# A new order of preparation work beside the products of a two-layer Flamingo-style kernel

## The chip, the cores and the metric

The kernel runs on one core of one Trainium2 chip. The metric is device time in microseconds (us), the median of repeated runs of the whole program. The engines are TensorE (PE in the profile, its weight loads PEld), VectorE (DVE), ScalarE (ACT) and GpSimd (POOL); SyncE (SP) issues nearly all transfers.

## What is computed

Four batches of 512 tokens, 512 channels wide, pass through two layers. Layer 0 adds a cross attention over normalised scores and a GELU network whose weights are first rounded to a 4-bit format with one power-of-two scale for each block of 32. Layer 1 adds a causal attention of 16 heads and a gated network whose hidden vector goes through a Walsh-Hadamard transform.

```python
x = x + tanh(g_xattn[0]) * L0_xattn(layernorm(x), ctx)
x = x + tanh(g_ffn[0]) * (gelu(layernorm(x) @ q4(up) + b) @ q4(down) + b2)
x = x + tanh(g_xattn[1]) * softmax(mask(q k^T / sqrt(32))) v Wout^T
h = silu(n @ W1^T) * (n @ W3^T);  x = x + tanh(g_ffn[1]) * fwht(h) @ W2^T
```

The transform is moved onto the weights: W2 is transformed once instead of every hidden vector. Products are made of two-part numbers (`hi`, `lo`), so one product is two or three matmuls for each pair of tiles.

## The kernel before

**Stages.** The cross attention of layer 0 fills the first 119 us. Then come the GELU products, `ffn0` (lines 579 to 632): the hidden dimension is cut into 16 chunks of 128 in four groups of 512 (`wq4[n]` holds one group's rounded weights, and two groups fit at a time). A call `ffn0(groups, b, beside)` runs the chunks of these groups for batch `b`: for each chunk eight `pu` matmuls (line 135), two GELUs on ACT, the subtraction `glo` on DVE (line 617), and for the chunk before it eight `acc` matmuls (line 594). The last 16 chunks are in `ffn0_end` (from 1026), where PE's order is the order of the program (`manual_schedule`). Then the attention of layer 1 in 16 units of four heads (loop over `s`, from 1573, one step `s` a head), and the gated network in 16 steps `n` (from 1797), in both of which PE keeps the program's order too. Elsewhere, and on all other engines, a planner orders instructions: it simulates the program with its own costs and gives each engine the earliest traced instruction that it believes ready.

**Work beside the products.** Preparations are Python generators. `work(k, jobs)` runs the next `k` steps of the first generator in a list. In `ffn0` each chunk runs `beside[0]` steps of `weight_jobs` and `beside[1]` of `jobs`, inside `with behind(traced())`: each instruction made there may not stand on its engine ahead of that engine's last instruction so far. That holds for PE, DVE, ACT and POOL; transfers are not held.

**Rounding.** `quantise(n)` (485 to 569) rounds group `n` in 11 steps: one that issues the loads of the raw weights into two half tiles `qw0` and `qw1`, one for each half that finds block scales (line 525 and a tree of maxima at 531), then four pairs of steps that round a quarter each (549 to 559). After the second and fourth pair a half is stored to `qw_d` (566). The next group's loads into a half wait for that store. `fetch_q(n)` (571) loads the rounded group back from `qw_d` as `up_q` and `dn_q`.

**W2 transform.** `hadamard_w2(c)` (953) takes ten steps for a quarter of W2: a load into `fw`, eight butterfly steps (an addition and a subtraction on DVE, lines 283 and 284), a store to `w2_d`. Two tiles `fw0` and `fw1` alternate, so the next quarter's first butterfly needs its own load and the store before it. `last_weights` (five steps) transposes Wq with PE, ACT and DVE. `preparations()` (1083) strings these together: four steps of quarter 0, rounding of group 2, the rest of quarter 0, rounding of group 3, `last_weights`, quarters 1 to 3: 62 steps in all.

**`ffn0_end`.** A list `plan` tells for each of the 16 chunks which jobs run before and after the chunk's `acc` matmuls: `A` is the first attention unit (queries of batch 0, then the largest scores of unit 0), `B` the queries of batch 1, `C` those of batch 2, `W` the preparations. The queries begin with a layer norm: statistics and scale on DVE (a step), the first rows `xn_c` on ACT (line 243, a step), then PE transposes (259), four steps.

**Attention.** `maxima(n)` (394) finds each row's largest score: score matmuls (410), for the two narrow row blocks with a mask added by a matmul (415) and one reduction (419), for the wide ones one reduction with mask for each head (423); then `mhi` on ACT and a transpose `pm` (435), whose rows are sent to the stacked operands. It is 13 steps, 11 of them scores. The narrowest row block takes four heads in its first step. Three steps run in each `s`; unit `u = (s + 7) // 4` starts where `k = (s + 7) % 4` is 0. The operands of unit n + 3 are loaded two heads at a time, after heads 1 and 3 of unit n (`load_heads`, 321). The exponentials need the largest scores of their unit.

Once for each batch the sums of the exponentials go to memory and back as reciprocals (`shares`, 1449: `den_d`, `rden`, `rden_d`, `rows_d`); `divide` (1493) spreads them by a matmul `rep` (1498) and multiplies on DVE, and `finish` (1504) multiplies by Wout.

**Norms of the gated network.** `norm(b)` (1249) takes the statistics of `x[b]` (194, 195) and a scale by twelve small DVE instructions (207 to 223). `combine` (1257) needs them for its rows. Norms 0 and 1 are traced at `s = 52`, norms 2 and 3 at step `n = 6` of the gated network.

Of the kernel before, what the change touches and what calls it, by code (L numbers as in the profile page):

```python
# [42 lines left out]
def flamingo_kernel(  # L43
# [350 lines left out]
    def maxima(n, masks, bank, bank_m, junk, mr):  # L394

        qst, kst = stacks[n]
        mask, mx, tri = masks  # L400
        fin = small.tile([P, NT, 4], F32, tag="fin", name=f"fin{n}")
        junk = junk(f"junk{n}")
        for i in range(NT):
            w = (i + 1) * P
            per = max(1, 4 // (i + 1)) if i < 2 else 1
            for g0 in range(0, 4, per):
                sc = bank([P, per, w], f"sc{n}_{i}_{g0}")
                masked = per > 1
                for g in range(per):
                    nc.tensor.matmul(  # L410
                        sc[:, g, :], qst[:96, g0 + g, ts(i, P)], kst[:96, g0 + g, :w],
                        start=(g == 0 or not masked), stop=not masked,
                    )
                if masked:
                    nc.tensor.matmul(  # L415
                        sc[:, :, w - P :], tri[:, 0], tri[:, 1].unsqueeze(1).to_broadcast([P, per, P]),
                        start=False, stop=True
                    )
                    nc.vector.tensor_reduce(fin[:, i, g0 : g0 + per], sc, AX.X, ALU.max)  # L419
                    yield  # L420
                    continue
                for g in range(per):
                    nc.vector.tensor_tensor_reduce(  # L423
                        junk[:, :w], sc[:, g, :], mask[:, S - w :], 1.0, -3.0e38,
                        ALU.add, ALU.max, fin[:, i, g0 + g : g0 + g + 1],
                    )
                yield
# [12 lines left out]
        yield  # L440
# [16 lines left out]
    with ExitStack() as l0:  # L457
# [121 lines left out]
        def ffn0(groups, b, beside=(0, 0), between=None):  # L579
# [8 lines left out]
            chunks = [4 * n + j for n in groups for j in range(4)]  # L588

# [11 lines left out]
            for f in chunks:  # L601
# [19 lines left out]
                with behind(traced()):  # L621
                    work(beside[0], weight_jobs)
                    work(beside[1])
# [10 lines left out]
        with ExitStack() as xa:  # L634
# [289 lines left out]

            def fetched(n):
                fetch_q(n)
                yield
# [17 lines left out]
            ffn0((0,), 0, (2, 5))  # L945
# [4 lines left out]
        with ExitStack() as ff:  # L950
# [132 lines left out]
            def preparations():  # L1083


                q = [quantise(n) for n in range(NG)]
                h = [hadamard_w2(c) for c in range(ND)]
                last = last_weights()
                next(q[2])
                yield from some(4, h[0])  # L1090
                yield from q[2]
                fetch_q(2)
                next(q[3])
                yield from some(6, h[0])
                next(h[1])
                yield from q[3]
                fetch_q(3)
                yield from last
                yield from some(8, h[1])
                next(h[2])  # L1100
                yield from h[1]
                yield from some(8, h[2])
                next(h[3])
                yield from h[2]
                yield from h[3]

            weight_jobs.append(preparations())
# [6 lines left out]
            ffn0((2, 3), 0, (1, 0))  # L1114
# [16 lines left out]
            with tc.manual_schedule(engines={nc.tensor.engine}):  # L1131
# [13 lines left out]
    with ExitStack() as l1:  # L1145
# [187 lines left out]
        with ExitStack() as at:  # L1333
# [238 lines left out]
            with tc.manual_schedule(engines={nc.tensor.engine}):  # L1572
                for s in range(-3, 4 * last + 2):
# [32 lines left out]
                    for i in range(3):  # L1606
# [36 lines left out]
                    if s > 20 and s % 16 == 6:  # L1643
                        jobs.append(finish(n // NO - 1))
# [255 lines left out]
```

## Time and profile before

| | us |
|---|---|
| three runs | 1315.11, 1318.45, 1318.72 |
| median | 1318.45 |
| profiled execution, its own time | 1317.84 |
| its span, first to last instruction | 1316.1 |
| busy: PE, DVE, ACT, POOL | 1217.1, 844.9, 553.7, 354.6 |

The span is shorter than the time by 1.7 us, and the profiled execution is 0.6 us under the median. The mean granted TensorE clock is 0.963 of full speed. A timeline line reads: start, duration, engine, line of the kernel, operation, output and inputs, shape, count, and in brackets the idle time before it with what ended it. A waits line reads: who waited for whom, us in total, times, longest. A windows line reads: stretch, its length, busy us of PE, PEld, DVE, ACT and POOL with counts, granted clock, share of DMA engines, GB/s.

### The profile page before, as it was taken

To read this page: it belongs to the slowest core of one execution; us is meant where nothing else is said; L and a number is where in the kernel's file an instruction comes from. 1 tells how busy PE (TensorE), PEld (TensorE's weight loads), DVE (VectorE), ACT (ScalarE), POOL (GpSimd) and SP (SyncE) were. 2 spreads that over 40 slices of the span, in tenths; PEclk is the share of its full clock that TensorE was granted. 3 is DMA by queue.
4 is the path that set the end of the run, shared out by engine and by line. 5 is a ranking of instruction groups with operands and counts; after the bars stand their busy time and mean duration, and the time that the engine had idled before them with its cause. 6 is when DMAs were issued, how large, how long until landed. Compare 5 with 4: busy or idle time off the path is not lost. (4 is left out here: it accounts for less than half of the span.)

```text
span 1316.1 us, 17489 instructions
## 1 busy us (share of the span) xinstructions
PE 1217.1 (92%) x6081; PEld 910.2 (69%) x6081; DVE 844.9 (64%) x1756; ACT 553.7 (42%) x1040; POOL 354.6 (27%) x480
## 2 busy tenths in 40 slices
PE   5998799998898899897999788999999999999998
PEld 4645577886676775464655466777777788888886
DVE  4977888795567674464564468666666755455556
ACT  4559642333423454444463755333334642222210
POOL 0000020000000133444444325344444533333330
PEclk9999899998899899899988989999999999999999
DMA  9792273713224565445341027344453644543421
GB/s 185 285 245 95 88 168 56 201 49 96 88 92 125 178 191 149 119 122 151 90 147 38 10 82 288 132 170 177 176 192 130 246 176 146 180 162 144 146 87 64
DMA packets 113202, 186.43 MB, mean 142 GB/s; under 512 B 13228, under 2 KB 65580, under 8 KB 107994
## 3 DMA queue, kind: packets, MB, share of 16 engines
q1 hardware_dynamic: 110754, 185.04, 44.7%
q8 instruction: 48, 0.79, 0.2%
q10 hardware_dynamic: 2360, 0.28, 0.2%
q14 instruction: 40, 0.33, 0.1%
HBM read 109.22 MB, written 75.80 MB: 141 GB/s over the span
## 5 line engine op out<-in xcount | busy, mean ns | idle before, releaser
L135 PE MATMUL pS<-tok,pack 128*128 128x512 f32 x768 | 195.0, 399 | 0.0
L135 PE MATMUL acc<-w2T,gg 128*128 128x512 f32 x768 | 182.1, 391 | 0.6 <-DVE x L1774 0.5
L135 PEld LDWEIGHTS pS<-tok,pack 128*128 128x128 f32 x768 | 142.7, 189 | 32.9
L135 PEld LDWEIGHTS acc<-w2T,gg 128*128 128x128 f32 x768 | 143.3, 188 | 31.8 <-DVE x L1774 1.9
L135 PE MATMUL pA<-tok,pack 128*128 128x512 f32 x576 | 149.7, 397 | 0.0
L135 PE MATMUL pu<-xnT,up_q 128*128 128x512 f32 x512 | 136.1, 411 | 7.4 <-DMA up_q<-qw_d 5.5
L1774 DVE SCALAR_TENSOR_TENSOR x<-acc,tg,x 128x512 f32<-128x512 f32 x128 | 96.2, 751 | 67.7 <-PE acc L135 67.4
L1392 ACT ACTIVATE e<-sT 128x384 f32<-128x384 f32 (+1 forms) x192 | 95.5, 527 | 75.2 <-PE sT L1388 72.9
L135 PEld LDWEIGHTS pA<-tok,pack 128*128 128x128 f32 x576 | 106.7, 188 | 23.8
L135 PEld LDWEIGHTS pu<-xnT,up_q 128*128 128x128 f32 x512 | 99.7, 197 | 32.4 <-DMA up_q<-qw_d 5.9
L1398 POOL TENSOR_SCALAR_AFFINE_SELECT e<-e 128x128 f32<-128x128 f32 (+1 forms) x192 | 63.2, 331 | 151.6 <-ACT e L1392 146.9
L423 DVE CUSTOM_DVE_ANT_0 junk<-sc,mask 128x384 f32<-128x384 f32 (+1 forms) x128 | 79.4, 620 | 27.8 <-PE sc L410 20.1
L410 PE MATMUL sc<-stk 96*128 96x128 f32 (+3 forms) x256 | 79.3, 359 | 11.8 <-DMA stk<-k_d 9.3
L1815 ACT CAST gg<-s 128x512 fp32r<-128x512 f32 x64 | 39.7, 621 | 108.5 <-POOL s L1812 95.7
L1812 POOL TENSOR_TENSOR s<-s,p 128x512 f32<-128x512 f32 x15 | 19.6, 1308 | 238.8 <-DVE p L1810 162.8
L1388 PE MATMUL sT<-stk 98*128 98x512 f32 (+3 forms) x256 | 78.1, 361 | 2.6 <-ACT e L1392 1.6
L594 PE MATMUL acc<-dn_q,glo 128*128 128x512 f32 x192 | 76.4, 398 | 3.8 <-DVE glo L617 3.8
L1816 POOL TENSOR_TENSOR gg<-s,gg 128x512 fp32r<-128x512 f32 x60 | 77.0, 1297 | 5.0 <-ACT gg L1815 4.8
L613 ACT ACTIVATE ghi<-pu,up_b 128x512 fp32r<-128x512 f32 x48 | 33.0, 688 | 103.9 <-PE acc L594 95.4
L594 PE MATMUL acc<-dn_q,ghi 128*128 128x512 f32 x192 | 75.9, 396 | 0.0
L419 DVE TENSOR_REDUCE fin<-sc 128x2 f32<-128x512 f32 (+1 forms) x48 | 32.6, 687 | 65.6 <-PE sc L415 65.3
L1388 PEld LDWEIGHTS sT<-stk 98*128 98x128 f32 x256 | 47.0, 199 | 30.9 <-issue 10.8
(291 smaller groups left out, 2226.4 us busy)
## 6 DMA issues: line engine op xcount, KB each, us to landing
pack_d<-pack SPq DMA_DIRECT2D x16, 1024.0 KB
pack<-pack_d SPq DMA_DIRECT2D x16, 1024.0 KB
pack_d<-pack SPq DMA_DIRECT2D x16, 768.0 KB
pack<-pack_d SPq DMA_DIRECT2D x16, 768.0 KB
qw_d<-qw SPq DMA_DIRECT2D x64, 128.0 KB
q_d<-qq SPq DMA_DIRECT2D x16, 512.0 KB
st<-in_L_ffn_W_dram SPq DMA_DIRECT2D x32, 256.0 KB
w2T_d<-w2T SPq DMA_DIRECT2D x16, 512.0 KB
```

Of the source, the lines that this page charges most:

```text
L135: nc.tensor.matmul(out, a, b, start=(i == 0), stop=(i == len(terms) - 1))
L410: nc.tensor.matmul(sc[:, g, :], qst[:96, g0 + g, ts(i, P)], kst[:96, g0 + g, :w], start=(g == 0 or not masked), stop=not masked,)
L419: nc.vector.tensor_reduce(fin[:, i, g0 : g0 + per], sc, AX.X, ALU.max)
L423: nc.vector.tensor_tensor_reduce(junk[:, :w], sc[:, g, :], mask[:, S - w :], 1.0, -3.0e38, ALU.add, ALU.max, fin[:, i, g0 + g : g0 + g + 1],)
L594: nc.tensor.matmul(acc[t], g[:, ts(t, P)], dn[:, f % 4, :], start=(f == chunks[0] and i == 0), stop=(f == chunks[-1] and i == 1 and groups ...
L613: nc.scalar.activation(ghi, ph, AF.Gelu_apprx_tanh, bias=up_b[:, f : f + 1])
L1388: nc.tensor.matmul(sc[:, at_ : at_ + S - j * P], kst[:98, g, ts(j, P)], qst[:98, g, j * P :], start=True, stop=True,)
L1392: nc.scalar.activation(e[:, ds(EOFF[js[0]], w)], sc, AF.Exp)
L1398: nc.gpsimd.affine_select(diag, diag, [[0, len(js)], [1, P]], ALU.is_ge, 0.0, base=0, channel_multiplier=-1,)
L1774: nc.vector.scalar_tensor_tensor(x[b][:, t, :], acc, tg[:, 3:4], x[b][:, t, :], ALU.mult, ALU.add)
L1815: nc.scalar.copy(g[:, 0], s)
L1816: eng.tensor_sub(g[:, 1], s, f32(g[:, 0]))
```

## The change

1. The first `ffn0` call runs one step of the rounding of group 1 for each chunk instead of two. So four of its twelve steps (with the fetch) move into the third call, and `preparations` begins in the fourth.
2. `in_order` ties the preparations: each step's DVE instructions stand behind the last DVE instruction of the step before.
3. `preparations` has a new order: two steps of quarter 0, group 2, three steps of quarter 0, group 3, the rest of quarter 0, `last_weights`, then quarters 1 to 3, each followed by an empty step; 65 steps. The last `ffn0` call takes two steps for each of its first five chunks. `ffn0_end` has a new plan: no `W` before the fifth chunk, the first transposes of `A` a chunk later, `B` started two chunks earlier and its transposes in the tenth.
4. `maxima` takes heads 0 and 1 through all row blocks, then heads 2 and 3: 12 steps of scores, the narrowest block in pairs. The closing `mhi` and `pm` move by one third of an `s`.
5. The four `rep` products move on half an `s`, from (5, 1), (5, 2), (6, 1), (6, 2) to (5, 2), (6, 1), (6, 2), (7, 1) of `s % 16` and third; `finish` begins one `s` later.
6. `norm` stands behind what is traced before it, so its DVE instructions keep their traced place.

```diff
@@ maxima
-        for i in range(NT):
+        for g0, i in ((g0, i) for h in (0, 2) for i in range(NT) for g0 in ((h,) if i < 2 else (h, h + 1))):
             w = (i + 1) * P
-            per = max(1, 4 // (i + 1)) if i < 2 else 1
-            for g0 in range(0, 4, per):
...
+            per = 2 if i < 2 else 1
+            sc = bank([P, per, w], f"sc{n}_{i}_{g0}")
...
@@ ffn0
+            rates = beside[0] if isinstance(beside[0], tuple) else [beside[0]] * len(chunks)
...
-                    work(beside[0], weight_jobs)
+                    work(rates[chunks.index(f)], weight_jobs)
@@
+            def in_order(job):
+
+                last = []
+                while True:
+                    with behind(last):
+                        if next(job, job) is job:
+                            return
+                    last = [i for i in traced() if i.engine == nc.vector.engine]
+                    yield
@@
-            ffn0((0,), 0, (2, 5))
+            ffn0((0,), 0, (1, 5))
@@ preparations
                 next(q[2])
-                yield from some(4, h[0])
+                yield from some(2, h[0])
                 yield from q[2]
                 fetch_q(2)
                 next(q[3])
-                yield from some(6, h[0])
-                next(h[1])
+                yield from some(3, h[0])
                 yield from q[3]
                 fetch_q(3)
-                yield from last
-                yield from some(8, h[1])
-                next(h[2])
-                yield from h[1]
-                yield from some(8, h[2])
-                next(h[3])
-                yield from h[2]
-                yield from h[3]
-
-            weight_jobs.append(preparations())
+                for c in range(ND):
+                    yield from some(8 if c else 4, h[c])
+                    if c + 1 < ND:
+                        next(h[c + 1])
+                    yield from h[c]
+                    if c == 0:
+                        yield from last
+                    else:
+                        yield
+
+            weight_jobs.append(in_order(preparations()))
@@
-            ffn0((2, 3), 0, (1, 0))
+            ffn0((2, 3), 0, ((2, 2, 2, 2, 2, 1, 1, 1), 0))
@@ ffn0_end: (before, after) the acc matmuls of each chunk
-                        ([], [A]), ([], [A]), ([], [W]), ([W], [A]), ([A], [A, W]), ([A], [W]),
-                        ([A], [A, A, W]), ([A], [A, W]), ([A], [A, B, W]), ([A], [A, B, W]),
-                        ([A, B], [A, W]), ([A, B], [A, W]), ([A, B], [A, W, W]), ([A, B], [B, W, W]),
-                        ([A], [B, C, W, W]), ([A, B], [B, C, W, W]),
+                        ([], [A]), ([], [A]), ([], []), ([], []), ([], [A, W]), ([A], [A, W]),
+                        ([A], [A, B, W]), ([A, A], [A, B, W]), ([A], [A, W]), ([A], [A, B, W, W]),
+                        ([A], [A, B, W, W]), ([A], [A, B, W, W]), ([A], [A, B, W, W]),
+                        ([A], [A, B, W, W]), ([A, A], [B, C, W, W]), ([A, B], [B, C, W, W]),
@@ norm
-            mv, moment = moments(NT, f"g{b}")
-            for t in range(NT):
-                moment(t, x[b][:, t, :])
-            norms[b] = scaling(mv, f"g{b}", 1e-5)
+            with behind(traced()):
+                mv, moment = moments(NT, f"g{b}")
+                for t in range(NT):
+                    moment(t, x[b][:, t, :])
+                norms[b] = scaling(mv, f"g{b}", 1e-5)
@@ attention loop
-                        if k == 0 and i:
+                        if (k, i) in ((0, 0), (0, 2), (1, 0)):
                             next(sought, None)
-                        if i and s > 20 and s % 16 in (5, 6):
+                        if s > 20 and (s % 16, i) in ((5, 2), (6, 1), (6, 2), (7, 1)):
                             next(division)
...
+                    if s > 20 and s % 16 == 7:
+                        jobs.append(finish(n // NO - 1))
...
-                    if s > 20 and s % 16 == 6:
-                        jobs.append(finish(n // NO - 1))
```

More of the change, by code (lines that the diff above doesn't have):

```diff
@@ L402, in maxima @@
         junk = junk(f"junk{n}")
-        for i in range(NT):
+        for g0, i in ((g0, i) for h in (0, 2) for i in range(NT) for g0 in ((h,) if i < 2 else (h, h + 1))):
             w = (i + 1) * P
-            per = max(1, 4 // (i + 1)) if i < 2 else 1
-            for g0 in range(0, 4, per):
[L407 to L427, printed above, removed]
+            per = 2 if i < 2 else 1
+            sc = bank([P, per, w], f"sc{n}_{i}_{g0}")
+            for g in range(per):
+                nc.tensor.matmul(
+                    sc[:, g, :], qst[:96, g0 + g, ts(i, P)], kst[:96, g0 + g, :w],
+                    start=(g == 0), stop=(per == 1),
+                )
+            if per > 1:
+                nc.tensor.matmul(
+                    sc[:, :, w - P :], tri[:, 0], tri[:, 1].unsqueeze(1).to_broadcast([P, per, P]),
+                    start=False, stop=True
+                )
+                nc.vector.tensor_reduce(fin[:, i, g0 : g0 + per], sc, AX.X, ALU.max)
+            else:
+                nc.vector.tensor_tensor_reduce(
+                    junk[:, :w], sc[:, 0, :], mask[:, S - w :], 1.0, -3.0e38,
+                    ALU.add, ALU.max, fin[:, i, g0 : g0 + 1],
+                )
+            yield
         hi = small.tile([P, NT, 4], FR, tag="mhi", name=f"mhi{n}")
@@ L1093, in preparations @@
                 next(q[3])
-                yield from some(6, h[0])
-                next(h[1])
+                yield from some(3, h[0])
                 yield from q[3]
                 fetch_q(3)
-                yield from last
-                yield from some(8, h[1])
-                next(h[2])
-                yield from h[1]
-                yield from some(8, h[2])
-                next(h[3])
-                yield from h[2]
-                yield from h[3]
-            weight_jobs.append(preparations())
+                for c in range(ND):
[5 more added lines that the diff above has]
+                        yield from last
+                    else:
+                        yield
+            weight_jobs.append(in_order(preparations()))
             ffn0((0,), 2, (1, 0))
```

## The prediction

> **What bounds the kernel now.** I read the page first, then the stretches of the stages, then PE's waits, then the timeline around each wait.
>
> ```profile
> PE 1217.1 (92%) x6081; PEld 910.2 (69%) x6081; DVE 844.9 (64%) x1756; ACT 553.7 (42%) x1040; POOL 354.6 (27%) x480
> PEclk9999899998899899899988989999999999999999
> ```
>
> PE is the bound, and DVE, at 64%, comes next. What can be won is PE's idle time and the stretches with a low clock. The stages, by windows (cross attention, `ffn0`, `ffn0_end`, attention, gated network):
>
> ```profile
> 0.00:118.80 118.80, 97.12 (x386) 60.43 (x386) 83.82 (x255) 69.43 (x153) 6.37 (x12) 0.96 0.82 222
> 118.80:336.00 217.20, 202.32 (x861) 159.72 (x862) 171.07 (x321) 93.34 (x155) 9.86 (x19) 0.96 0.42 105
> 336.00:448.00 112.00, 97.68 (x432) 77.50 (x431) 76.62 (x175) 41.60 (x67) 3.15 (x10) 0.94 0.40 122
> 448.00:776.00 328.00, 291.52 (x2018) 186.82 (x2017) 182.07 (x482) 171.89 (x349) 130.66 (x273) 0.92 0.38 111
> 776.00:1316.10 540.10, 528.46 (x2389) 425.72 (x2389) 331.27 (x526) 177.48 (x318) 204.61 (x167) 1.00 0.44 161
> ```
>
> PE idles 14.9, 14.3 and 36.5 us in the second to fourth stage, and only 11.6 in the long fifth. PE's waits by releaser (180 to 460 us, then 455 to 780):
>
> ```profile
> PE pt_c L259 <- ACT xn_c L243: 9.4, 2, 4.9
> PE pu L135 <- DMA up_q<-qw_d: 5.5, 1, 5.5
> PE acc L594 <- DVE glo L617: 2.6, 2, 2.3
> ...
> PE sc L410 <- DMA stk<-k_d: 9.3, 6, 3.9
> PE rep L1498 <- DMA rows_d<-rden_d: 6.0, 3, 2.3
> ```
>
> PE's timeline at some of them:
>
> ```profile
> 318.04 2.50 PE L135 MATMUL pu<-xnT,up_q 128*128 128x512 f32 x5 [5.47 <-DMA up_q<-qw_d]
> ...
> 350.62 1.11 PE L259 MATMUL pt_c<-ident,xn_c 128*128 128x128 f32 x4 [4.49 <-ACT xn_c L243]
> 351.38 3.76 PE L135 MATMUL pu<-xnT,up_q 128*128 128x512 f32 x8
> ...
> 358.27 2.11 PE L135 MATMUL pu<-xnT,up_q 128*128 128x512 f32 x8
> ...
> 604.90 0.41 PE L410 MATMUL sc<-stk 96*128 96x128 f32 x2 [3.88 <-DMA stk<-k_d]
> ```
>
> Eight `pu` matmuls take 3.76 us right after a wait and 2.11 later: a wait costs some 1.7 us more by the clock. DVE's timeline shows who is late:
>
> ```profile
> 199.13 1.23 DVE L525 TENSOR_SCALAR qc<-qw 128x2048 int16<-128x2048 int16 x1 [5.07 <-DMA qw<-n_L_ffn_down_kernel_dram]
> ...
> 305.18 1.22 DVE L559 TENSOR_TENSOR qw<-qc,qcols 128x1024 f32<-128x1024 bf16 x1
> ...
> 798.73 1.19 DVE L212 SCALAR_TENSOR_TENSOR rs_g<-rs_g,var_g 128x4 f32<-128x4 f32 x1
> ```
>
> **The change part by part**, against the profiled 1317.84 us.
>
> *Rounding and W2 (`ffn0`).* Group 3's rounding is 28 us of DVE (two scale halves of about 3, four quarters of 5.3), spread over nine chunks of 3.7 us that also hold a `glo` (0.65) and a quarter of the update of x (0.66): 40 us of work in 33. Before, butterflies of quarter 1 and Wq's subtractions (some 8 us between 294 and 305) ran in between, so it ended at 306.4, its store began then, and `up_q` landed 11.6 us later, at 318.04. Tied, those stand behind it: the end comes near 290 to 296 and the weights land by 308, while PE wants them at 312.6. The wait goes: 5.47 + 1.75 = **7.2**. What is late next there is nothing: the call after it has its group.
>
> Group 1 pays. Its last quarter ended at 179.8; now it is held behind the third chunk's `glo` of the third call (181.75 + 0.6) and takes 2.9, so it ends at 185.3 or later, say 186. All its eight stores, the two fetches and group 2's eight loads of the second half move with it on SP's queue, which is in order (behind them stand W2's and Wq's loads, not urgent; POOL's queue issues none). `up_q` lands at 186 + 11.6 = 197.6, and PE's first product with it stood at 197.9. Bounds: no wait, or the whole slip of four chunks (14.7), which makes 8.2 + 1.75. I take **-1.5**, near the first end, because the row gives the earliest place. Group 2's second half landed 19.3 us after group 1's end, so at 205; its L525 then stands near 201 and DVE waits about as before. That wait held `glo` and cost PE 2.31 and 1.4 of clock at 202; one chunk of the two that PE runs ahead is now spare, so half goes: **1.9** (bounds 0 and 3.7). PE's 4.30 us before 148.94 waited for `xnT` L122 behind DVE work of which line 557 (0.60) and 556 (0.3) move away: **0.9** (bounds 0 and 6). The last call's two steps for a chunk are 2 x 1.3 us of DVE (line 283 and 284, 0.69 each) beside 1.3 for `glo` and the update: 3.9 in a chunk of 3.7. PE's lead of a chunk or two covers it, and I take 0; if that cover is gone it costs what the wait at 202 cost, 3.7. Together **8.5**.
>
> *`ffn0_end`.* The two first transposes waited 4.49 and 4.88 us for rows that hung on a scale (DVE) late behind butterflies. A later place by one chunk (3.7), with no butterflies ahead (2.4 us at 343.8 to 346.9), covers the first; three chunks in place of one and a half cover the second. With clock 1.75 and 1.2: 12.3. But quarter 3's first butterfly now comes one chunk (4.6) after its load instead of two: the load issued at 393.07 was used at 406.81. Nothing shows how long it needs; between 0 and 9 us of DVE wait, of which PE keeps half a chunk spare. I take -2.3. Together **10.0**.
>
> *Pairs of heads.* Six `sc` waits of 9.28 us fall on the first step, which needed heads 2 and 3. Now these are wanted on the seventh step, more than one `s` (2.4 us at least) later. Three waits (2.22, 0.55, 3.88) go, two with clock loss (1.75 each): 10.15. The other three (1.44, 1.02, 0.17) stand just before the `rep` waits of 1.75, 2.26 and 1.96, whose transfer chain (`den_d` issued at 537.5, landed at 547.2) starts from an unmoved place. PE only reaches the same transfer sooner; half an `s` there holds about 0.75 us of other matmuls. So 3 x 0.75 = 2.2, not 8.6, and the clock loss stays. Cost: a further weight load (0.098) and DVE reduction (two of 256 columns, by the nearest rows 0.41 each, for one of 0.69) for 15 units: -1.5. `pm` and its four transfers on SP still come more than one `s` before their exponentials, and only the next operand loads stand behind them: 0. `finish` one `s` later frees three waits of 0.53 for `oT`, and its products only change place: 0, at best 1.6. Together **10.9**.
>
> The Trainium skill ("TensorE: Matmul & The Clock Gate", Part 1) has the clock halve only after an idle window of about 3.4 us. The trace disagrees: a wait of 1.36 us before 670.85 is followed by a granted clock of 0.50 for 675 to 680. By the page's window the two waits of 2.2 to 2.3 us would bring no clock loss, and the sum would be 1.75 + 0.7 = some 2.5 us smaller.
>
> *Norms.* Norm 3 holds DVE from 783 to 800 in pieces, and its last links (798.73 and beside it) delay L1200, whose bank PE awaits for 2.45 us before 801.50: 2.0. Norm 2 between `combine`'s rows costs waits of 0.57 and 0.63: 1.2. Both norms come back at step 6, 5.4 us of DVE each (4 x 0.69, 4 x 0.18, 12 x 0.16) in a stretch (976 to 1010) where DVE is busy 23.2 of 34: room for 10.8. Bounds 0 and 4 (four PE banks of 1.4 cover most of a burst): -1.0. Norms 0 and 1 move from 563 to 666 to behind `s = 52`, near 695, where DVE is busy 3.29 of 12 us, and `combine` asks for them from `s = 56` on: 0, and without that cover a wait like the 1.37 at 731.96 with its clock loss, 3.1. Together **2.2**.
>
> The sum is 31.6. Everything off PE is planned anew, and each stretch at DVE's limit may bring a small wait that no row shows; by the two `glo` waits of 2.6 us in all in this stage I take off 2.6 us. So **29** less: 1317.84 - 29 = 1289, and the median stands 0.6 above the profiled run, which changes nothing. **1289**.
>
> **The rivals.**
>
> *The tied rounding lands late in part (1304).* Group 1's weights come one or two chunks late (8.2 + 1.75), and W2's swaps make DVE wait at both later quarters (about 2.5 us of PE each): 15 us back. For it: the row at 199.13, where the planner believed a load landed 5 us early. Against: group 1's earliest place is only 6 us later.
>
> *Waits only move (1318).* The pairs and the plan uncover the next transfer (`rep`, the swap of `fw`), and the planner had the ties anyway, so that they do nothing. For it: the three `rep` waits behind the `sc` waits. Against: 3.88, 4.49, 4.88 and 5.47 have nothing behind them.
>
> *Slower (1326): DVE stands in front of transfers.* Tied steps leave it nothing to put in between. Five places: the second halves of groups 2 and 3 and three swaps of `fw`. The row at 199.13 is the price of one: 5.07 us of DVE cost PE 3.7 with the clock. Five of those give 1289 + 18.5 = 1307. It decides when each costs PE over 6 us, which is about 8 us of DVE waiting each; at 8 of PE each it is 1289 + 40 = 1329, less the 2.6 already set aside: 1326. Against: a whole fetch behind stores took 11.6, and most places have a chunk or more between.
>
> **How the numbers follow.** Likeliest case 0.55, with its own range 1277 to 1301 (down: 5 more at 148.94, 1.8 at 202, 2.3 at the swap and the 2.6 set aside; up: 8.5 more for group 1 and 3 for the norms). Late in part 0.20, waits only move 0.07, slower 0.18. Faster by over 0.3% (4 us, about what a measurement can tell) holds the first two: 0.75; same 0.07; slower 0.18. The range 1275 to 1320 leaves out the slower case and a little at the low end.
>
> **What would show it.** Right: no `up_q` wait after 300 us, last L559 before 298; no `xn_c` waits of PE; `sc <- stk` near 0 and `rep <- rows_d` at 6 us or more; `st_g` of norms 2 and 3 only after 970 us; gated network 2 to 3 us shorter before 820. Wrong: a `pu` wait near 200, DVE idle on `fw` or `qw` loads above 5 us in several places, or new PE waits on DVE at 980 to 1010.

## The result, and the profile after

| | before | after |
|---|---|---|
| median, us (16 runs each, side by side) | 1318.15 | 1327.56 |
| lowest and highest | 1309.48, 1326.09 | 1318.91, 1333.19 |
| ratio of the times, 95% interval | | 1.0069 (1.0046 to 1.0092) |
| profiled execution, its own time | 1317.84 | 1333.19 |

The change makes the kernel 0.7% slower, some 9 us, where 29 us less were forecast. The profiled execution of after is the slowest of its 16, 5.6 us over the median, so its stages can't be added up to 9 us. PE's busy time and its clock, from the page:

```profile
PE 1234.5 (93%) x6097; PEld 923.7 (69%) x6097; DVE 849.5 (64%) x1772; ACT 550.9 (41%) x1040; POOL 354.8 (27%) x480
PEclk9998899989999899787978789999998999999999
```

PE is busy 17 us longer with 16 more instructions: most of that is a lower clock. The windows of `ffn0`, `ffn0_end`, attention and gated network (stretch, length, busy PE, PEld, DVE, ACT, POOL, clock, share of DMA, GB/s):

```profile
118.80:336.00 217.20, 199.70 (x846) 157.69 (x847) 168.78 (x316) 93.32 (x157) 9.63 (x19) 0.95 0.40 101
336.00:448.00 112.00, 101.03 (x450) 79.92 (x449) 83.19 (x196) 43.96 (x72) 3.51 (x11) 0.95 0.46 137
448.00:776.00 328.00, 300.54 (x2026) 195.28 (x2025) 175.94 (x460) 167.40 (x347) 129.53 (x271) 0.87 0.38 108
776.00:1331.50 555.50, 536.55 (x2393) 431.42 (x2392) 337.71 (x545) 178.29 (x318) 205.68 (x168) 0.99 0.43 157
```

In `ffn0` PE idles more than before (17.5 us for 14.9). In the attention it idles less (27.5 for 36.5), but the clock falls from 0.92 to 0.87. In the gated network it idles 19 us where it idled 11.6. PE's waits in the stretches 180 to 480, 455 to 800 and 780 to 1340 us:

```profile
PE acc L592 <- DVE glo L615: 5.5, 2, 4.0
PE pu L135 <- DMA up_q<-qw_d: 4.2, 2, 3.0
PE pt_c L259 <- DVE fin L418: 2.9, 2, 2.6
...
PE sT L1397 <- DMA stk<-mr: 5.0, 4, 3.6
PE sT L1397 <- ACT mr L434: 4.6, 5, 2.3
...
PE ph L135 <- DVE hs L122: 9.2, 3, 3.6
```

All waits that the change aimed at are gone or smaller: `xn_c` (9.4 before, 0.2 after, not among these lines), `sc` for `stk` and `rep` for `rows_d` (9.3 and 6.0 before, neither in the view now), `up_q` after 300 us (5.47, now 3.0). Three stand in their place: `glo` (2.6 before), `mr` (none before) and `hs` (2.3 before in this stretch). PE's timeline at the largest of them:

```profile
268.24 0.79 PE L592 MATMUL acc<-dn_q,glo 128*128 128x512 f32 x1 [4.02 <-DVE glo L615]
318.22 3.62 PE L135 MATMUL pu<-xnT,up_q 128*128 128x512 f32 x8 [3.00 <-DMA up_q<-qw_d]
609.87 0.77 PE L1397 MATMUL sT<-stk 98*128 98x512 f32 x1 [3.63 <-DMA stk<-mr]
1020.07 0.72 PE L135 MATMUL ph<-hs,had 128*128 128x512 f32 x2 [3.60 <-DVE hs L122]
1029.23 1.22 PE L135 MATMUL ph<-hs,had 128*128 128x512 f32 x2 [3.62 <-DVE hs L122]
```

DVE's timeline behind the first and the last:

```profile
209.10 1.23 DVE L522 TENSOR_SCALAR qc<-qw 128x2048 int16<-128x2048 int16 x1 [6.39 <-DMA qw<-n_L_ffn_down_kernel_dram]
...
265.63 1.23 DVE L522 TENSOR_SCALAR qc<-qw 128x2048 int16<-128x2048 int16 x1 [8.29 <-DMA qw<-n_L_ffn_down_kernel_dram]
...
1012.54 2.46 DVE L194 BATCH_NORM_STATS2 st_g<-x 128x6 f32<-128x512 f32 x4
...
1020.99 1.35 DVE L207 TENSOR_SCALAR rs_g<-var_g 128x4 int32<-128x4 int32 x2
1022.30 1.27 DVE L211 TENSOR_TENSOR rs_g<-rs_g 128x4 f32<-128x4 f32 x2
1023.53 1.28 DVE L212 SCALAR_TENSOR_TENSOR rs_g<-rs_g,var_g 128x4 f32<-128x4 f32 x2
...
1028.49 0.68 DVE L122 TENSOR_TENSOR hs<-pw,hs 128x512 fp32r<-128x512 f32 x1
```

Both held-back norms run between 1012.54 and 1028.5, and the two `hs` that PE needs next stand among and behind them. Pairs of `rs_g` instructions take 1.27 to 1.35 us; two such instructions elsewhere take 0.24. POOL's timeline at that place:

```profile
1020.95 1.29 POOL L1821 TENSOR_TENSOR s<-s,v 128x512 f32<-128x512 f32 x1 [0.24 <-DVE var_g L221]
1022.20 2.51 POOL L1825 TENSOR_TENSOR gg<-s,gg 128x512 fp32r<-128x512 f32 x2
```

The ends fit each other. POOL's instructions end at 1022.24, 1023.48 (inside the second row) and 1024.71, DVE's pairs at 1022.34, 1023.57 and 1024.81. In each pair it is the first instruction that is long, 1.19 to 1.28 us, and it ends 0.02 us after POOL's; the second takes 0.15.

### The profile page after: what moved, and what is told of

The parts are those of the page before. It is cut to its first block, busy times and chain, and to the rows that moved or that the text cites. A ratio compares the mean times of both kernels' runs of the same rounds, so it can differ in the third digit from the quotient of the medians.

```text
span 1331.5 us, 17526 instructions
## 1 busy us (share of the span) xinstructions
PE 1234.5 (93%) x6097; PEld 923.7 (69%) x6097; DVE 849.5 (64%) x1772; ACT 550.9 (41%) x1040; POOL 354.8 (27%) x480
## 4 chain that ended last, share of the span: by engine, by line
PE 71%; DMA 12%; DVE 10%; ACT 5%; issue 2%; SPq 1%; POOL 0%; DVEq 0%; ACTq 0%; POOLq 0%
PE acc L135 13%; PE pS L135 13%; PE pA L135 10%; PE pu L135 6%; PE acc L592 4%; PE pp L140 4%; PE sT L1397 3%; PE sc L409 2%; PE den L1437 2%; PE pav L1429 2%; PE pq L140 2%; PE pq L135 1%; DMA dn_q<-qw_d 1%; DMA qw<-n_L_ffn_down_kernel_dram 1%; PE acc L1051 1%
## 5 line engine op out<-in xcount | busy, mean ns | idle before, releaser
L135 PE MATMUL pA<-tok,pack 128*128 128x512 f32 x576 | 153.0, 404 | 0.0
L420 DVE CUSTOM_DVE_ANT_0 junk<-sc,mask 128x512 f32<-128x512 f32 (+1 forms) x128 | 79.6, 622 | 96.3 <-PE sc L409 91.7
L1397 PE MATMUL sT<-stk 98*128 98x512 f32 (+3 forms) x256 | 86.5, 383 | 12.9 <-DMA stk<-mr 5.0
L409 PE MATMUL sc<-stk 96*128 96x128 f32 (+3 forms) x256 | 85.5, 377 | 2.1 <-ACT e L1401 1.0
L1397 PEld LDWEIGHTS sT<-stk 98*128 98x128 f32 x256 | 50.1, 213 | 48.4 <-issue 18.7
L611 ACT ACTIVATE ghi<-pu,up_b 128x512 fp32r<-128x512 f32 x48 | 33.1, 689 | 101.7 <-PE acc L592 99.5
L409 PEld LDWEIGHTS sc<-stk 96*128 96x128 f32 x256 | 50.0, 210 | 13.8 <-ACT e L1401 4.8
```

The source lines that it names most:

```text
L135: nc.tensor.matmul(out, a, b, start=(i == 0), stop=(i == len(terms) - 1))
L409: nc.tensor.matmul(sc[:, g, :], qst[:96, g0 + g, ts(i, P)], kst[:96, g0 + g, :w], start=(g == 0), stop=(per == 1),)
L420: nc.vector.tensor_tensor_reduce(junk[:, :w], sc[:, 0, :], mask[:, S - w :], 1.0, -3.0e38, ALU.add, ALU.max, fin[:, i, g0 : g0 + 1],)
L611: nc.scalar.activation(ghi, ph, AF.Gelu_apprx_tanh, bias=up_b[:, f : f + 1])
L1397: nc.tensor.matmul(sc[:, at_ : at_ + S - j * P], kst[:98, g, ts(j, P)], qst[:98, g, j * P :], start=True, stop=True,)
```

## The experiments

Ratios are against the kernel before, on the same chip, with 95% intervals; 0.0010 is 1.3 us. The last columns are lengths of stages in one profiled execution each, between milestones: `ffn0` (first to last `acc` of it), `ffn0_end` (to its last `acc`), attention (to the last `sT`), gated network (first to last update of x).

| kernel | ratio | `ffn0` | end | attention | gated |
|---|---|---|---|---|---|
| before | 1 | 211.7 | 101.7 | 307.6 | 490.6 |
| after | 1.0069 (1.0046-1.0092) | 212.4 | 94.2 | 312.5 | 503.1 |
| e1 norms as before | 0.9951 (0.9928-0.9973) | 215.1 | 93.8 | 306.9 | 490.5 |
| e2 closed early | 0.9999 (0.9979-1.0019) | 212.3 | 94.6 | 308.5 | 499.6 |
| e3 feed-forward part alone | 0.9962 (0.9943-0.9981) | 208.7 | 97.6 | 304.0 | 490.5 |
| e4 attention part alone, closed early | 0.9987 (0.9967-1.0007) | 212.0 | 102.1 | 307.9 | 490.5 |
| e5 = e1 + e2 | 0.9905 (0.9872-0.9938) | 211.4 | 94.6 | 306.4 | 490.9 |
| e6 pairs alone | 1.0012 (0.9988-1.0036) | 214.7 | 102.4 | 306.8 | 490.8 |
| e7 quotients alone | 0.9976 (0.9951-1.0001) | 212.4 | 101.9 | 302.4 | 491.3 |
| e8 norms apart | 1.0067 (1.0037-1.0096) | 212.5 | 94.2 | 308.9 | 504.0 |
| e9 e3 without ties | 1.0091 (1.0062-1.0119) | 225.9 | 98.6 | 307.2 | 490.6 |
| e10 gate on DVE | 1.0025 (0.9996-1.0055) | 206.8 | 93.5 | 308.2 | 498.5 |
| e11 norms in pieces | 1.0028 (0.9999-1.0057) | 211.9 | 94.2 | 306.9 | 500.7 |
| e12 e3 + quotients | 0.9976 (0.9949-1.0004) | 215.5 | 98.5 | 308.4 | 490.5 |
| e13 = e5 again | 0.9883 (0.9851-0.9914) | 211.9 | 93.2 | 304.7 | 490.8 |
| e14 e13 with the old first rate | 0.9949 (0.9919-0.9978) | 208.7 | 101.0 | 303.3 | 490.8 |
| e15 e3 + pairs | 0.9924 (0.9896-0.9952) | 207.6 | 93.5 | 307.1 | 490.7 |
| e16 = e12 again | 0.9937 (0.9907-0.9967) | 210.1 | 96.6 | 305.2 | 490.6 |

How firm a column is shows where the code is the same: the gated network with the norms as before is 490.5 to 491.3 in 13 kernels; `ffn0` of the change is 206.8 to 215.5, the attention scatters by 4 us and more. So what the change does in `ffn0` and in the attention is told by the ratios, and in `ffn0_end` and the gated network also by the stage. The columns leave out two stretches that scatter as much: the time up to the first `acc` (122.0 to 132.6 us) and that from the last `sT` to the first update of x (72.8 to 78.4).

**e1 and e2: the two suspects undone one by one.** e1 takes `norm`'s tie away:

```diff
-            with behind(traced()):
-                mv, moment = moments(NT, f"g{b}")
+            mv, moment = moments(NT, f"g{b}")
...
```

> The changed kernel with `norm` as it was before (not tied to the last instructions of other engines), all else changed. Theory (the norms 2 and 3 now come in one burst of VectorE work between 1012 and 1029 us, and PE stands 3.60 and 3.62 us for `hs` behind it, with a clock of 0.74 in that stretch): the burst goes, the two waits of `ph` for `hs` go, and the time falls by 9 to 12 us to about 1316 to 1318. The norms come back into 783 to 800 us and cost there the 2 to 3 us that they cost before. Rival (the waits near 1020 come from the order of the other work of that step, which the earlier stages have shifted): `ph` still waits for `hs` near 1020 and the time stays within 3 us of 1327.

1312.5, 15.6 us less than after by the ratios, more than the 9 to 12 expected; the gated network is 12.6 us shorter, and PE's waits for `hs` beyond 800 us fall from 9.2 to 2.3. So the held-back norms cost more than the whole loss, and the rest of the change gains 6 us.

e2 closes the maxima as early as their last reduction allows:

```diff
-                        if (k, i) in ((0, 0), (0, 2), (1, 0)):
+                        if (k, i) in ((0, 0), (0, 1), (0, 2)):
```

> The changed kernel with the maxima closed in the three steps of one slot, as early as the pairs allow (the last reduction, the rounding of the maxima and their transposition at (k, i) = (0, 0), (0, 1), (0, 2) in place of (0, 0), (0, 2), (1, 0)). Theory (the later place brings PE's nine waits of `sT` for `mr`, 5.0 us for its transfer and 4.6 us for its scaling on ScalarE, and with them a lower clock): these waits go, no other takes their place, and the time falls by 8 to 13 us to 1315 to 1320. Rival (PE only reaches the `rep` transfers or the exponentials of ScalarE sooner): waits of `rep` for `rows_d` come back at 5 to 6 us in all, and the time falls by 0 to 4 us.

9.2 us less by the ratios, as the theory said. The waits of `sT` for `mr` are gone, but others come, against the theory; `rep`, which the rival named, is not among them (0.3 us). PE's waits in the attention (448 to 800 us):

```profile
PE sT L1397 <- ACT e L1401: 6.2, 13, 3.1
...
PE pm L432 <- ACT mx L427: 2.7, 11, 0.6
```

And the clock of the stage is only 0.89. Where it is lost shows in windows of 2 us:

```profile
528.00:530.00 2.00, 1.38 (x7) 0.75 (x5) 1.71 (x7) 1.42 (x4) 1.16 (x3) 1.00 0.47 128
530.00:532.00 2.00, 1.98 (x9) 1.62 (x9) 0.97 (x3) 1.28 (x3) 1.45 (x4) 0.64 0.09 28
532.00:534.00 2.00, 2.00 (x9) 1.02 (x12) 0.96 (x4) 1.13 (x3) 1.24 (x5) 0.50 0.76 216
534.00:536.00 2.00, 2.00 (x16) 0.40 (x8) 1.44 (x5) 0.00 (x0) 0.71 (x1) 0.50 0.69 194
```

Here the clock is halved for some 6 us, and the waits ahead of it are 0.21, 0.16 and 0.48 us.

**e3 and e4: the parts alone.** e3 is the kernel before with `in_order`, the new `preparations`, rates and plan of `ffn0_end`; e4 is it with the new `maxima`, the moved quotients and `finish`, closed early as in e2. (`ffn0_end`'s plan gives e4 one more step of `A` in its last chunk but one, since the maxima have one step more.)

> The kernel before with the feed-forward part of the change alone (tied steps, new preparations, new rates, new plan of `ffn0_end`). Theory by the two traces (the calls of `ffn0` end 3.5 us later against before, `ffn0_end` is 7.5 us shorter by its own stage, later stages as before): 4 us less than before, so 1314. Rival (the prediction's terms, -8.5 and -10.0): 1300. In the trace: VectorE stands over 5 us for the second half of group 2 and again of group 3 (`qc` for `qw`), and `up_q` of group 3 still makes PE wait some 3 us near 318.

> The kernel before with the attention part alone (largest scores by pairs of heads, quotients half a slot on, `finish` one step later), but the maxima closed at (k, i) = (0, 0), (0, 1), (0, 2). Theory (the prediction's working of this part was right but for the late closing): the `sc` waits for `stk` (9.3 us) go, the `rep` waits stay near 6 us, no `sT` waits for `mr`, and the time is 8 to 11 us below before, so 1307 to 1310. Rival (the pairs only move waits, and cost a further weight load and reduction in each unit): within 3 us of before.

e3: 5 us less, as the two traces said. e4: 1.7 us less, an interval that holds zero; the rival was right. The `sc` waits are gone and those of `rep` fall to 1.9, where 6 was expected, and yet the attention is no shorter (307.9 for 307.6).

**e5 to e7: do the parts add?** e6 is e4 without the moved quotients and `finish`, e7 those alone.

> The changed kernel with both suspects undone: `norm` as before and the maxima closed in the three steps of one slot. Theory (the two losses are separate, and add): the ratio of 0.9951 with the norms back, times the 0.9999/1.0069 that the early closing gave, is 0.988, so about 1303. Rival (the early closing gave time only where the norms stood, and the attention part is worth nothing): the feed-forward part alone, 0.996, so about 1313.

> The kernel before with only the largest scores by pairs of heads, closed early; quotients and `finish` where they were. Theory A (the pairs' gain is real, and the moved quotients ate it): the `sc` waits for `stk` go, and the time is 6 to 10 us below before, 1309 to 1313. Theory B (PE only runs into ScalarE's exponentials sooner: the removed waits return as many small waits of `sT` for `e`, and the clock is as low as before or lower): within 3 us of before, clock of the stretch 448 to 748 at 0.88 to 0.92, waits of `sT` for `e` above 4 us in all against 1.6.

> The kernel before with only the quotients' steps half a slot on and `finish` one step later. Theory A (this move costs what the pairs gain): 4 to 8 us above before. Theory B (it takes away some 2 us of waits of `oT` and `rep`, and nothing else): 0 to 3 us below before. In the trace: `rep` for `rows_d` falls from 6.0 us to under 3, `pp` for `oT` from 2.5 to near 0.

e5 gives 1307.7 and beats both kernels. e6 gains nothing. Its waits of PE in the attention, 448 to 800 us (before: `rep` 6.0, `sT` for `e` 1.6):

```profile
PE rep L1495 <- DMA rows_d<-rden_d: 7.6, 3, 3.4
PE sT L1385 <- ACT e L1389: 3.9, 14, 0.6
PE pm L432 <- DVE rs_g L212: 2.5, 1, 2.5
```

Some 8 of the 9.3 us are there again under other names (1.6 of them are `pm` for `mx`, not among these lines). e7: the `pp` waits for `oT` are gone, but `rep` did not fall (7.7) as was expected; the time may be 3 us less, at the edge of what can be told.

**e8, e10, e11: why do held-back norms cost so much?** e8 puts norm 2 at n = 2 and norm 3 at n = 4:

```diff
-                    if n == NN - 2:
-                        jobs.extend([norm(2), norm(3)])
+                    if n in (2, 4):
+                        jobs.append(norm(2 + n // 4))
```

> The changed kernel with the held-back norms 2 and 3 put at two different steps of the gated network (n = 2 and n = 4) in place of both at n = 6; all else changed. Theory (the cost is the burst: 10.8 us of both norms stand together ahead of one `hs`, in a stretch where VectorE has little room): each norm alone delays PE by 1 us at most, so the time falls by 9 to 13 us to about 1315 to 1318. Rival (holding a norm behind an instruction of its step costs some 5 us wherever it stands): the time stays within 3 us of 1327. Small instructions of the norms (`rs_g`, 0.16 us each) that last over 1 us beside an instruction of POOL: if the traces show them here too, they belong to POOL and not to the burst.

My theory of the double burst fell: the time is that of after. PE's timeline:

```profile
868.92 0.72 PE L135 MATMUL ph<-hs,had 128*128 128x512 f32 x2 [1.30 <-DVE hs L122]
874.77 0.73 PE L135 MATMUL ph<-hs,had 128*128 128x512 f32 x2 [1.90 <-DVE hs L122]
...
945.07 0.72 PE L135 MATMUL ph<-hs,had 128*128 128x512 f32 x2 [1.84 <-DVE hs L122]
951.81 1.22 PE L135 MATMUL ph<-hs,had 128*128 128x512 f32 x2 [2.79 <-DVE hs L122]
```

Each norm alone makes PE wait twice, at either place. And 11 of the norms' small instructions there last 0.73 to 1.28 us; each of the 11 ends within 0.05 us of the end of a POOL instruction.

e10 is after with the gate of two steps taken from POOL:

```diff
-                        eng = nc.vector if n == 2 * NN - 1 else nc.gpsimd
+                        eng = nc.vector if n in (NN - 3, NN - 2, 2 * NN - 1) else nc.gpsimd
```

> The changed kernel, but at n = 5 and n = 6 the gate's multiplication and subtraction, which POOL has at 1.28 us each, are done by VectorE (0.69 us each); the held-back norms stay. Theory (a small instruction of VectorE on two operands in SBUF stands until the instruction that POOL is in has ended; so the norms at n = 6 take 4.4 us more than their own time): no `rs_g` instruction after 1000 us lasts over 0.3 us. For the time: VectorE has 5.5 us more work in each of the two steps and 4.4 less of standing, so it stays within 4 us of 1327. Rival (the long small instructions have another cause, such as the queue of VectorE itself): some of them stay at 1.2 us with POOL empty.

POOL is empty from 995 to 1032 us, and no small instruction of the norms lasts over 0.17 us. DVE's timeline of e10:

```profile
1022.30 0.23 DVE L211 TENSOR_TENSOR rs_g<-rs_g 128x4 f32<-128x4 f32 x2
1023.48 0.23 DVE L212 SCALAR_TENSOR_TENSOR rs_g<-rs_g,var_g 128x4 f32<-128x4 f32 x2
1023.67 0.24 DVE L213 SCALAR_TENSOR_TENSOR rs_g<-rs_g,rs_g 128x4 f32<-128x4 f32 x2
```

So the long ones are POOL's doing. The time is 6 us below after, more than the 4 allowed for, although DVE has more to do. But 8.0 of the 12.6 us that the held norms cost in the gated network remain (498.5 against 490.5): PE still waits 3.95 us for `hs` at 1019.06, behind four statistics of the other norm and the gate's work.

e11 cuts both norms into ten held pieces, one in each half of n = 2 to n = 6:

```diff
+            mv, moment = moments(NT, f"g{b}")
+            for t in range(NT):
+                with behind(traced()):
+                    moment(t, x[b][:, t, :])
+                if b > 1:
+                    yield
             with behind(traced()):
-                mv, moment = moments(NT, f"g{b}")
-                for t in range(NT):
-                    moment(t, x[b][:, t, :])
                 norms[b] = scaling(mv, f"g{b}", 1e-5)
...
+                        if k == 4 and 1 < n < NN - 1:
+                            next(held)
```

> The changed kernel with norms 2 and 3 held back in ten pieces, one in each half of the steps n = 2 to n = 6 (a moment of one tile, 0.85 us, in eight of them; the scaling with its 14 small instructions in two). Theory (what costs is a long block of VectorE work ahead of one `hs`, made longer by POOL): the pieces of 0.85 us cost nothing, the two scalings some 2 to 3 us each beside POOL, so the time is 5 to 10 us below the changed kernel's 1327. Rival (every held piece costs its own length, because the fixed order of PE has no slack anywhere): within 3 us of 1327.

5.4 us below after, the low end of the theory. Beyond 800 us PE still waits 5.8 us for `hs` in six pieces (one of 2.0 is there in after too) and newly 4.5 for x in eight. Four of these pieces, 0.73 us each, follow the held moments in the second halves of the steps. So even 0.85 us of held DVE work ahead of PE's fixed order costs.

**e9 and e14: why `ffn0` gained nothing.** e9 is e3 without the tie:

```diff
-            weight_jobs.append(in_order(preparations()))
+            weight_jobs.append(preparations())
```

> The kernel before with the feed-forward part alone, but without the tie from step to step (`preparations()` goes into the list as it is; its new order, the rates and the new plan of `ffn0_end` stay). Theory (the tie is what makes VectorE stand 6.4 and 8.3 us for the second halves of groups 2 and 3, because nothing may be put in between; the gain is that of the later transposes in the plan of `ffn0_end`): VectorE's waits of `qc` for `qw` shrink by half or more, and the time is 0 to 4 us below the tied version's 1314. Rival (the tie brings the gain, because without it butterflies of later steps stand in front of the rounding): the second half of group 3 ends later, PE's wait for `up_q` near 318 grows above 5 us, and the time is 3 to 8 us above 1314.

The rival was right, and by more than it said: 17 us above e3. PE's waits from 120 to 440 us:

```profile
PE pu L135 <- DMA up_q<-qw_d: 14.9, 1, 14.9
```

Without the tie eight instructions of W2's butterflies stand among the last quarter's steps, and it ends at 317.4 us (305.9 in after). So the tie does what it was meant to do. It is not what makes DVE stand: without it DVE still waits 6.27 and 5.15 us for the second halves of groups 2 and 3, where e3 has 5.98 and 8.03. What remained had another cause, which e14 tests in the version of e13, by giving the first call its old rate:

```diff
-            ffn0((0,), 0, (1, 5))
+            ffn0((0,), 0, (2, 5))
```

> The version of e13 with two weight steps for each chunk of the first call in place of one, as before the change. Theory (group 1's rounding ends at 187 to 188 us in place of 179.8, and on SP's queue, which is in order, group 2's and group 3's loads follow by the same 7 to 8 us; so VectorE stands 8 us for group 3 and PE 3.0 for `up_q` near 318): group 1 ends 6 to 8 us earlier, VectorE's wait near 265 falls below 3 us, PE's waits for `up_q` (1.2 and 3.0) and for `glo` near 268 (4.0) go, and the time is 5 to 9 us below e13's. Rival (the rounding of group 3 is bound by its own steps, one in a chunk, not by its load): the loads come earlier but the wait for `up_q` stays, and the time is within 2 us of e13's.

The chain is as the theory said: group 1 ends at 181.7 (188.3 in after), and all waits for `up_q` are gone. But DVE's wait for group 3 only falls to 6.78, where under 3 was expected, and PE still waits 3.73 us behind it, for x at 261.42. DVE's timeline, with the last step of group 3's rounding, and below it the same place in the kernel before (line 525 there):

```profile
257.23 1.23 DVE L522 TENSOR_SCALAR qc<-qw 128x2048 int16<-128x2048 int16 x1 [6.78 <-DMA qw<-n_L_ffn_down_kernel_dram]
...
294.60 1.23 DVE L556 TENSOR_TENSOR qw<-qc,qcols 128x1024 f32<-128x1024 bf16 x1
```

```profile
259.48 1.23 DVE L525 TENSOR_SCALAR qc<-qw 128x2048 int16<-128x2048 int16 x1 [0.18 <-DMA w_d<-fw]
```

The second half of group 3 comes some 20 us after the rounding of group 2 has ended: at 265.6 after 245.5 in after, at 257.2 after 235.7 in e14. The kernel before used it at 259.5, 21.6 us after that end, and did not wait for it; it has six steps of W2 between the two roundings, where the new order has three. With less work in between DVE gets there sooner and stands. That the missing steps are the reason was not tested by itself.

The rounding now ends at 295.8, yet the kernel is 9 us slower than e13: `ffn0` is 3 us shorter and `ffn0_end` 8 longer (a wait of 3.02 for `xn_c` at 358.5 is back), which is where its plan meets preparations that are four steps further on. What of that makes up the 8 us was not tried. The two columns make 5 of the 9 us; where the rest lies is not shown.

**e13, e15, e16: pairs and quotients beside the feed-forward part.**

> The changed kernel with `norm` as before and the maxima closed early (feed-forward part, pairs, quotients), a second time, beside the two versions that lack one part of it. Theory (the parts of the attention are worth something only together): 0.990 to 0.993 again. Rival (its first measurement was low by chance): 0.995 to 0.997.

> The version of e13 without the moved quotients and `finish`. Theory (only together): 0.995 to 0.998, as the feed-forward part alone. Rival A (the pairs carry the gain): 0.990 to 0.993. In the trace: without the moved quotients `rep` waits for `rows_d` 7 us or more, with them under 3.

> The version of e13 without the pairs, a second time, on this chip. Theory (only together): 0.995 to 0.998, as in its first measurement (0.998). Rival B (the quotients carry the gain): 0.990 to 0.993.

e13 confirms e5: 1303.3, the fastest measured. The pairs are worth 5 us or more beside the feed-forward part (e15 against e3, e13 against e16), where they were worth nothing alone. So the first rival of e15 was right, though `rep` waits only 3.9 us there, not 7. e12 was expected at 0.994, or 0.9905 if the pairs only move waits, and missed both. The column of `ffn0_end` says where some 3.5 us of the pairs' worth lie: 101.7 to 102.4 in the old plan with or without pairs, 96.6 to 98.6 in the new plan without them, 93.2 to 94.6 with them (e14 apart). In this stage the first unit's scores are made, and the new plan is cut for their twelve steps. The quotients' share lies within the scatter (e12 and e16, the same code, are 0.004 apart).

## Why the prediction was wrong

**Norms: forecast -2.2, measured +12 to +16** (after against e1; e2 against e5 and e13). The step that failed is "room for 10.8 ... four PE banks of 1.4 cover most of a burst", bounds 0 and 4. I counted DVE's free time in the stretch from 976 to 1010, as if any of it would do. But the work is held ahead of one instruction, `hs`, whose product comes next in PE's written order; free time after it is no cover. And 10.8 us was no length for the two norms in that place: four pairs of their small instructions stood 4.3 us more beside POOL's gate. The row was there: the one at 798.73, 1.19 us for an instruction that I costed at 0.16 elsewhere, and I read it as an ordinary delay. Of the expected gain before 820 us little is seen: PE waits 4.1 us between 790 and 810 instead of 5.2, and the first update of x comes 1.9 us later after the last `sT`, in a stretch that differs by 4.5 us between e5 and e13, the same code.

**Pairs of heads: forecast -10.9, measured -1.7 alone (e4), -7.5 and -10.4 beside the feed-forward part (e5 and e13 against e3), all closed early.** Three steps failed. "`pm` and its four transfers on SP still come more than one `s` before their exponentials, ...: 0" is wrong: the closing moved a third of an `s` nearer to them, and the `sT` waits for `mr` (9.6 us) are its price, 6 to 9 us by e1, e2, e5 and e13. "Have nothing behind them" was wrong of the 3.88: behind the `sc` waits stood ACT's exponentials, for which PE now waits, in many small pieces (e2, e6). And "a wait costs some 1.7 us more by the clock" was taken as saved with the wait. That did not come: the stage's clock is 0.89 to 0.92 with the pairs closed early, 0.92 before, though PE idles less in most of these runs, and in e2 small waits stand ahead of a halved clock. Without the pairs it is 0.89 to 0.94, so how much of the clock hangs on them is not shown. The rival that waits only move, at 0.07, described this part. What the pairs do bring I had in no step: some 3.5 us in `ffn0_end`.

**Rounding and W2: forecast -8.5, measured about nothing (-1.4 in the length of `ffn0`, as the mean of twelve kernels with it against four without, with a scatter of 2.5).** "Group 1 pays ... say 186" was right: 188.3, in an execution whose `ffn0` begins 2.8 us later. So was "DVE waits about as before" for group 2: 6.39 us, with 5.07 in the kernel before and 7.1 to 7.6 in e4, e6 and e7, which have the old code here; PE lost 1.45 at it. What failed is the step after that. The wait for group 3's second half had no term: DVE stands 8.29 us, and PE 4.02 behind it. With this and the slip of group 1, the rounding ends at 305.9 in place of 290 to 296, and of the `up_q` wait of 5.47 the kernel keeps 3.0. With group 1 early (e14) the rounding ends at 295.8, inside the forecast, and the wait for `up_q` is gone, so that step was right as far as it went. The 4.30 at 148.94 is 4.55 now; no part of it was the work that moved away.

**`ffn0_end`: forecast -10.0, measured -8.** Right in mechanism: the two `xn_c` waits are gone. Half of it needs the pairs. The swap of `fw`, for which I took off 2.3, came about as forecast. DVE stands for it, the reduction `fin` comes behind it, and PE's transposes wait for that:

```profile
403.52 0.69 DVE L283 TENSOR_TENSOR fw<-fw 128x512 f32<-128x512 f32 x1 [2.83 <-DMA w_d<-fw]
405.34 0.68 DVE L418 TENSOR_REDUCE fin<-sc 128x2 f32<-128x512 f32 x1
406.17 0.63 PE L259 MATMUL pt_c<-ident,xn_c 128*128 128x128 f32 x4 [2.56 <-DVE fin L418]
```

In e14, where DVE does not stand there, no such wait of PE is longer than 0.41. Waits of transposes for `mv_c` and `xnT_late`, 3.6 us together, were there before (3.4).

**The sum.** Feed-forward part with pairs and quotients, closed early: -12.5 and -15.4 (e5, e13). The late closing takes 6 to 9 of it, the norms 12 to 16. That gives +3 to +13, and +9 was measured. Along the path e5, e1, after this comes out by construction; that the norms cost 12 to 16 with either closing is what shows that the two losses add. The slower rival had the sign, but not the reason. Of its five places at 8 us each, two cost PE something new, 4.02 (group 3) and 2.56 (the swap), and the feed-forward part alone still gained 5 us (e3). The largest loss was at a place that no rival named, though "new PE waits on DVE at 980 to 1010" was on the list of signs, some 10 us early.

## What to carry to other kernels

Free time on an engine covers held work only if it comes before the next instruction that a fixed order elsewhere needs; count from there, not over a window. A wait removed from an engine that runs close behind another one can come back in pieces, as PE's for ACT did here. Parts of a change that re-plans several stages are worth measuring alone: here the held norms and the later closing cost more than the rest gained, and the version without them is 0.9 to 1.2% faster than before.

## What the runs showed of the hardware

**A small DVE instruction can stand until the POOL instruction beside it has ended.** The norms' instructions on four columns (`var_g`, `rs_g`), 0.16 us elsewhere, lasted up to 1.29 us where they met a POOL instruction of 1.28, and ended 0.01 to 0.03 us after it; with POOL empty (e10, from 995 us on) none did. The same norms' statistics (0.66 to 0.70 us), and instructions with an operand in PSUM, kept their time beside POOL. Larger ones show the same: additions on 256 columns took 0.41 to 0.42 us beside POOL with one operand in PSUM (L1218, L1219), and up to 1.46 with both in SBUF (L1221, L1222; after and e8). The Trainium skill ("SBUF — State Buffer", "SBUF: two separate sides") describes this as a port pair that the two engines share and that one of them holds for its whole instruction. The traces agree, down to the ends of the instructions, and show that the price is a matter of POOL's length, not of DVE's.

**The clock can halve after small waits, but mostly does not.** In e2 waits of 0.21, 0.16 and 0.48 us within 3 us were followed by 0.50 for some 6 us. I had tied the low clock to single waits of 1.4 us and more. The profile gives the clock in pieces of 3.4 us. In all 18 traces from 120 us on, a piece at full clock in which PE idled 2 us or more was followed by a halved one every time (131 of 131). With 0.25 to 1 us of idle time it was so for 61 of 283 pieces in the attention and for 7 of 158 elsewhere, none of them in the gated network. What else decides is not shown. The Trainium skill ("TensorE: Matmul & The Clock Gate", "A second HAM failure mode: psum-queue depth-cycling") tells of another kernel whose clock swings from short idle times between groups of matmuls; this stage is a second case, and its waits have their length beside them.
